# The order of a one-core attention kernel: a written table in place of a scheduler

## The chip, the cores and the metric

The kernel runs on one core of one Trainium2 chip. The metric is the device time of a run in microseconds, as the median of three runs. One profiled execution of the kernel before gives the page, the timelines and the groups of instructions quoted below. A core has five instruction queues that matter here: TensorE (PE, with its weight loads PEld), VectorE (DVE), ScalarE (ACT), GpSimd (POOL) and SyncE (SP). SP issues nearly all transfers of this kernel. Each queue runs its instructions in the order in which the program lists them, and each waits by semaphores for what it needs.

## The reference

Inputs are x of 2 x 2048 x 640, read as four sequences of 512 tokens of 640, and ctx of 2 x 128 x 384, read as four sequences of 81 tokens of 384, of which the last four are adapter tokens. All is float32, with 8 heads of 80.

```
query = x @ Wq;  keyt = enc @ Wk;  valt = enc @ Wv          # enc: the first 77 tokens, ca: the last 4
hs = mha(query, keyt, valt)
ca_q1 = einsum('btc,th->bch', ca, Wq_ca)[:, indices]        # indices = linspace(0, 383, tokens)
ca_hs1 = mha(ca_q1, x, x)
ca_hs2 = mha(ca_hs1 @ Wq, ca @ Wk_ca, ca @ Wv_ca)
out = (hs + ca_hs2) @ Wout + b_out + x
```

mha is softmax attention with scores scaled by one over the square root of 80. In the kernel the inputs are handled as two batches b of 2048 rows, with 124 keys in a padded form for the text and 384 rows of the adapter path, which a gather spreads over the tokens at the end.

## The kernel before, in words

The kernel is written as tasks. A task is a Python generator that yields operations, `Do(engine, fn, after, needs, frees, marks)`: the engine that issues it (or two engines to choose from), the function that emits its instructions, the events it waits for, the buffers it takes from a `Room`, the buffers it gives back, and the events that it marks. It can also yield a `Fork`, which begins another task. `Desk` (line 65) lists the operations in an order, calls each `fn` in turn, and pins the instructions in program order. So the order in which operations are listed is the order on each engine's queue. Instructions of DVE, ACT and POOL have the helper's line 284, PE products line 254, transposes line 269, and SP's transfers line 304.

Before the change that order is worked out when the program is built. `Desk.run` (line 205) takes, again and again, the operation that can start first by `Desk`'s own estimates of durations and landings. Among those that can start at once it takes the lowest rank: the task's rank, plus a correction from the table `RANKS`, plus a price for a change of PE's form of tile. `Room.take` hands out the buffers that came free earliest by the estimates. Where an operation may run on two engines, the one that would start it first gets it.

PE products with more than 64 rows and more than 64 columns are split by `matmul` (line 248) into four strips of 32 columns, "128*32" in the profile, unless PE is in the whole form "128*128" just then. Each float32 product of a strip shows as two records.

The work has these stages.

- First loads, weights, transposes, keys and values (to about 75 us). `keys` sends k_parts out to DRAM and reads them back in other places; `x_load(b, sb, after)` loads the eight blocks of x, `yz_block(b, sb)` makes from each the adapter's z and y, and `wq_turned` and `sums_of_wq` prepare weights.
- `adapter(b)`: for each batch 24 score products s on PE. Each is read by a maximum on DVE (mx<-s) in the first pass and by exponentials on ACT (ea<-s) in the second, and then contracted with y (acc). `second(b)` makes the adapter's second attention from that: a softmax of four on DVE and ACT, a transpose (pt_p) and a copy p2T, and then, for three blocks of 128 rows, two products (po<-w_sb,p2T), two copies o<-po on ACT, and a store o<-o by SP. p2T and the o2 tiles come from `eas`, a room of two. When second(1) is done, four PSUM banks more join the four of `banks`.
- `queries(n)` and `queries_fast(n)`: the query products pq, the later ones in a form with sums, `x_sums` and `wq_sums`, that needs fewer products. Some partial results (`rests`) go through DRAM by "away" and "landing" transfers.
- `text(m)` for 16 units m of two row tiles each: `text_scores` (sc), `softmax` on DVE, ACT and POOL (m, p, r, and the share p<-p,r on "POOL or DVE"), a DVE transpose eb, and a store kept<-eb to DRAM. `probabilities(m)` (line 1937) takes one of two pT buffers from `pTs` and reads the probabilities back in four transfers pT<-kept, each for 32 partitions. `text_out_fast` (line 2091) then does three hidden products ph (c0 = 0, 2, 4), each copied to hs by ACT or DVE. The last one gives the pT buffer back. Four sums of hs on DVE or POOL follow, and four `sums_chain` tasks with the output products po, each added by DVE onto the residual row buffer.
- `residual(m)` (line 2027) loads the two row tiles of x into two of eight row buffers (x_more and last_rows), by SP. `stored(m, k, ...)` (line 2205) runs when a tile is complete: POOL adds the adapter's rows by an indirect transfer (line 2049), and SP stores the tile, after which its row buffer is free. Tiles finished before second(b) is done are put aside to DRAM ("early") and read back later.

Each SP transfer stands in one queue with all others. A load into a buffer that an earlier transfer or product still reads makes SP wait, and with it whatever is listed behind. The lines around such a load are these:

```
op = yield Do("NONE", lambda z: wide("pT", z[0], f"pT_{m}"), needs=[(pTs, 1)], marks=[("back", m)])
for j in range(4):
    op = yield Do("SP", lambda: dma(pT[R * j : R * (j + 1)]..., by_keys[j], 1.1),
                  [("kept", m, 0), ("kept", m, 1)], rank=0)
...
op = yield Do("SP", load, [("back", m)], needs=[(rows, 1)])     # residual(m): one of two row tiles
```

Of the kernel before, what the change touches and what calls it, by code (L numbers as in the profile page):

```python
# [14 lines left out]
P = 128  # L15
# [4 lines left out]
class Event:  # L20


    def __init__(self):
        self.t = None


class Room:


    def __init__(self, n):  # L30
        self.at = [0.0] * n

    def when(self, n):
        free = sorted(t for t in self.at if t is not None)
        return free[n - 1] if len(free) >= n else None

    def take(self, n):
        order = sorted((t, i) for i, t in enumerate(self.at) if t is not None)[:n]
        for _, i in order:
            self.at[i] = None  # L40
        return [i for _, i in order]


class Do:
# [4 lines left out]
    def __init__(self, engine, fn, after=None, needs=(), frees=(), marks=(), rank=None, mode=None):  # L49
        self.engines = (engine,) if isinstance(engine, str) else engine  # L50
        self.fn, self.after, self.needs, self.frees = fn, after, needs, frees
        self.marks, self.rank, self.slots, self.value, self.mode = marks, rank, [], None, mode


class Fork:
    def __init__(self, gen, rank):
        self.gen, self.rank = gen, rank


class Task:  # L60
    def __init__(self, gen, rank, more):
        self.gen, self.rank, self.more, self.last = gen, rank, more, Event()


class Desk:
# [3 lines left out]
    ENGINES = ("PE", "ACT", "DVE", "POOL", "SP", "NONE")  # L69
    WHOLE, WIDE, SWITCH, LEAVE, ANOTHER = (P, 32), (P, None), 18.4665, -14.8473, 39.005  # L70
    START = {(P, P): 0.06, (64, P): 0.107, (P, 64): 0.107, (64, 32): 0.03, (P, 32): 0.03}
    DRAIN = {
        ((P, P), (32, P)): 0.136, ((P, P), (64, P)): 0.095, ((P, P), (P, 32)): 0.093,
        ((32, P), (P, 32)): 0.06, ((P, P), (P, P)): 0.0,
    }
    DRAINS = {(64, P): 0.148, (32, P): 0.108, (P, 32): 0.1}
    MORE = {
        "v_transpose": 0.025, "v_stream_shuffle": 0.09, "v_scalar_tensor_tensor": 0.07, "v_reciprocal": 0.035,
        "a_activation": 0.045,
    }  # L80
    COLD = 5.2
    TAIL = {"PE": 0.25, "DVE": 0.18, "ACT": 0.2, "POOL": 0.25, "SP": 0.1, "NONE": 0.0}


    RANKS = {
        "adapter": {(1,): -11.4},
        "chain": {(2, 0): 6, (2, 1): 10, (2, 2): -2, (2, 3): 19, (3, 0): -3, (3, 1): 21, (3, 2): -2, (3, 3): -2,
            (4, 1): -1, (4, 2): -0.6, (5, 0): -6, (5, 1): 20, (5, 2): -4, (5, 3): 3, (6, 0): -1, (6, 1): 16,
            (6, 3): -17, (7, 0): -3.1, (7, 1): -39.6, (7, 2): -4, (7, 3): -25},
        "context": {(): -4},  # L90
        "contract": {(0, 0): 5.7, (1, 0): -0.3, (1, 1): 5},
        "first_halves": {(): 2},
        "first_loads": {(): 1},
        "gather_rows": {(): -5},
        "halves_away": {(1,): 0.7, (3,): -1.3, (4,): 10, (5,): -2, (7,): -5},
        "keys": {(): 1.6},
        "load_wout": {(): -13},
        "probabilities": {(0,): 0.2, (1,): -4.7, (2,): -6, (3,): 7, (4,): 24.6, (5,): 11, (6,): 8.2, (7,): -23,
            (8,): 21.5, (9,): 27.1, (10,): -19.8, (11,): 25.9, (12,): 3, (13,): 16, (14,): 24.8,
            (15,): 24.7},  # L100
        "queries": {(0,): 1, (1,): -0.1},
        "queries_fast": {(2,): 36, (3,): -13, (4,): 20, (5,): 11.1, (7,): -19.7},
        "residual": {(1,): 20, (2,): -14, (3,): -1.7, (4,): -21, (5,): -8, (7,): -16, (8,): 3, (11,): 4, (13,): 15,
            (14,): 5},
        "rest_back": {(0,): 6, (1,): 20, (2,): -8.8, (3,): -10, (4,): 4, (5,): 38, (8,): 8, (10,): 10, (11,): -18.2,
            (12,): -24, (13,): 7, (14,): 2, (15,): 0.7},
        "second": {(0,): -25},
        "softmax": {(0, 0): -17.3, (0, 1): -4, (1, 0): -9, (2, 0): -7, (5, 0): -12.7, (5, 1): -20, (6, 0): -1.6,
            (6, 1): 2.1, (7, 0): -18, (7, 1): 4, (8, 0): -19, (9, 0): 8.6, (9, 1): 0.7, (10, 0): 28,
            (10, 1): 6, (11, 0): -1, (11, 1): -11.7, (12, 1): -3, (13, 0): -4, (13, 1): 10, (14, 0): -1.4,  # L110
            (15, 0): 10, (15, 1): -19},
        "stored": {(0, 0): 21, (0, 1): 12, (1, 0): -8, (1, 1): 7.2, (2, 1): 13, (3, 0): -6, (3, 1): -15, (4, 0): 2,
# [3 lines left out]
        "sums_chain": {(0, 0): -12.8, (0, 1): -4, (0, 2): 1, (0, 3): -2.3, (1, 0): -12, (1, 1): 20, (1, 2): 1.9,  # L116
# [7 lines left out]
        "sums_of_wout": {(): -2},  # L124
        "sums_of_wq": {(): 2},
        "text": {(1,): 7, (2,): -23, (3,): 12.8, (4,): 6, (5,): -10, (6,): 0.9, (7,): -1, (8,): -10, (9,): 2,
            (11,): 2.5, (12,): 11.1, (14,): -20.7, (15,): -5},
        "text_scores": {(0,): 19, (1,): -6, (2,): -17.3, (3,): 1, (5,): -10, (6,): -1, (7,): -15.8, (9,): -14,
            (12,): 6.7, (14,): 1.5, (15,): 5},
        "text_values": {(): 17},  # L130
        "values_weights": {(): 21},
        "wq_turned": {(): 4.2},
        "x_first": {(): 1},
        "x_load": {(0, 2): -4.4, (1, 1): 16, (1, 2): -20, (1, 3): 11},
        "y_rows": {(0, 0): 8, (0, 1): 16.8, (0, 2): -13, (0, 3): 34.1, (1, 0): 15, (1, 1): 8, (1, 2): -10,
            (1, 3): -1},
        "y_weights": {(): -6},
        "yz_block": {(0, 0): -40, (0, 1): -21, (0, 2): -6, (1, 0): -0.5, (1, 1): -16, (1, 2): -17, (1, 3): -22},
        "z_weights": {(): 4.9},
    }  # L140

    def __init__(self, tc):
        self.tc, self.nc, self.now, self.spent, self.mode = tc, tc.nc, 0.0, 0.0, None
        self.free = {e: 0.0 for e in self.ENGINES}
        self.queue = {e: [] for e in self.ENGINES}
        self.events, self.landed, self.channel, self.log = {}, 0.0, 0.0, []
# [4 lines left out]
    def known(self, key):  # L151
        return self.event(key).t is not None

    def begin(self, gen, rank):
        frame, key = gen.gi_frame, []
        for arg in frame.f_code.co_varnames[: frame.f_code.co_argcount]:
            if type(frame.f_locals[arg]) is not int:
                break
            key.append(frame.f_locals[arg])
        task = Task(gen, rank, self.RANKS.get(gen.__name__, {}).get(tuple(key), 0.0))  # L160
        task.last.t = self.now
        self.go_on(task, None)

    def go_on(self, task, value):
        while True:
# [6 lines left out]
            value = self.begin(op.gen, op.rank)  # L172
        op.task, op.at = task, Event()
        op.wait = [task.last] if op.after is None else [self.event(k) for k in op.after]
        op.order = task.rank if op.rank is None else op.rank
        task.last = op.at
        for e in op.engines:
            self.queue[e].append(op)

    def change(self, mode):  # L180


        if mode == self.WIDE:
            mode = self.mode if self.mode == (P, P) else self.WHOLE
# [126 lines left out]
def kernel(  # L311
# [30 lines left out]
    G = 32  # L342
# [1956 lines left out]
```

## Time and profile before

| what | value |
|---|---|
| runs | 587.95, 586.0, 587.6 us; median 587.6 |
| profiled execution | 588.24 us, its span 586.5 us |
| mean granted clock of PE | 0.997 |
| PE busy | 571.5 us, 97% of the span |
| DVE, ACT, POOL busy | 403.7, 279.1, 153.2 us |
| share of PE in the chain that ended last | 78% |
| DMA | 115.29 MB, 197 GB/s in the mean |
| SP's transfers | 64 loads pT<-kept, median 7.2 us from issue to landing; stores of rows 7.3 and 7.7 us |

How to read what is quoted. A row of the busy time by stretch gives the stretch, its length, then the busy time and the number of instructions of PE, PEld, DVE, ACT and POOL, the clock granted to PE, the share of the DMA engines and GB/s. A row of a timeline gives start, length, engine, line, operation, "out<-in", tile form (PE: rows*columns of the array that a product uses), shape and number of instructions; in brackets stands the idle time just before it and what ended it. A row of the groups gives the busy time and the mean of one in ns, and then the idle time before them. A row of the waits gives the waiting engine and line, what it waited for, the us in total, the number of times and the longest. A row of the transfers gives their number, KB each, and the median us from issue to landing.

### The profile page before, as it was taken

To read this page: it belongs to the slowest core of one execution; us is meant where nothing else is said; L and a number is where in the kernel's file an instruction comes from. 1 tells how busy PE (TensorE), PEld (TensorE's weight loads), DVE (VectorE), ACT (ScalarE), POOL (GpSimd) and SP (SyncE) were. 2 spreads that over 40 slices of the span, in tenths; PEclk is the share of its full clock that TensorE was granted. 3 is DMA by queue.
4 is the path that set the end of the run, shared out by engine and by line. 5 is a ranking of instruction groups with operands and counts; after the bars stand their busy time and mean duration, and the time that the engine had idled before them with its cause. 6 is when DMAs were issued, how large, how long until landed. Compare 5 with 4: busy or idle time off the path is not lost.

```text
span 586.5 us, 18596 instructions
## 1 busy us (share of the span) xinstructions
PE 571.5 (97%) x7913; PEld 301.2 (51%) x7913; DVE 403.7 (69%) x642; ACT 279.1 (48%) x764; POOL 153.2 (26%) x205
## 2 busy tenths in 40 slices
PE   9999999999999999999998999999999999999996
PEld 7474334545555645545544544455555564555553
DVE  2257789999999665487889999976366354444443
ACT  3132165645445789798324425269788721111110
POOL 7202031251516700000123314423213202322251
PEclk9999999999999999999998999999999999999999
DMA  8997756594868865334947999899968796799987
GB/s 274 182 247 132 155 123 205 148 201 127 161 183 168 207 147 178 103 108 151 218 129 193 281 296 229 188 270 258 293 191 168 210 257 145 185 259 260 261 173 198
DMA packets 153420, 115.29 MB, mean 197 GB/s; under 512 B 83317, under 2 KB 125685, under 8 KB 153338
## 3 DMA queue, kind: packets, MB, share of 16 engines
q1 hardware_dynamic: 147706, 103.42, 67.9%
q0 software_dynamic: 5632, 10.69, 11.0%
q8 instruction: 62, 1.02, 0.8%
q14 instruction: 20, 0.16, 0.1%
HBM read 72.54 MB, written 41.53 MB: 194 GB/s over the span
## 4 chain that ended last, share of the span: by engine, by line
PE 78%; DVE 9%; DMA 5%; ACT 5%; issue 2%; POOL 0%; SPq 0%; DVEq 0%; ACTq 0%
PE po L254 24%; PE pq L254 24%; PE ph L254 6%; PE sc L254 5%; PE s L254 5%; PE acc L254 5%; DMA kept<-eb 4%; PE pyz L254 2%; ACT ea L284 2%; DVE mx L284 2%; ACT p L284 2%; DVE eb L284 1%; PE pv L254 1%; PE pk L254 1%; DVE zop L284 1%
## 5 line engine op out<-in xcount | busy, mean ns | idle before, releaser
L284 DVE TENSOR_REDUCE mx<-s 128x4 f32<-128x2048 f32 x48 | 109.0, 2272 | 8.1 <-PE s L254 8.1
L284 ACT ACTIVATE p<-sc,m 128x124 f32<-128x124 f32 x256 | 89.9, 384 | 21.6 <-DVE m L284 21.0
L284 ACT ACTIVATE ea<-s 128x2048 f32<-128x2048 f32 x48 | 91.0, 1896 | 18.8 <-PE s L254 18.6
L254 PE MATMUL pq<-xt,wq_sb 128*32 128x256 f32 (+2 forms) x974 | 83.7, 428 | 0.0
L254 PE MATMUL po<-wout_sums,hs 128*32 128x320 f32 (+1 forms) x988 | 77.0, 433 | 0.0
L254 PE MATMUL po<-wout_sb,hs 128*32 128x320 f32 x944 | 76.0, 433 | 0.1
L284 POOL TENSOR_TENSOR p<-p,r 128x992 f32<-128x992 f32 x16 | 29.9, 1866 | 121.7 <-DVE r L284 121.7
L284 DVE TENSOR_TENSOR x_more<-x_more,po 128x320 f32<-128x320 f32 x68 | 32.3, 482 | 38.6 <-PE po L254 38.3
L284 ACT ACTIVATION_READ_ACCUMULATOR p<-sc,m 128x1 f32 x256 | 58.2, 227 | 0.0
L284 ACT COPY hs<-ph 128x512 f32<-128x512 f32 (+1 forms) x34 | 18.6, 547 | 82.3 <-PE ph L254 82.3
L254 PEld LDWEIGHTS pq<-xt,wq_sb 128*32 128x32 f32 (+1 forms) x974 | 35.6, 113 | 34.4 <-issue 18.9
L254 PE MATMUL acc<-ea,y_sb 128*32 128x384 f32 (+2 forms) x768 | 51.3, 385 | 0.0
L284 DVE TENSOR_TENSOR last_rows<-last_rows,po 128x320 f32<-128x320 f32 x60 | 28.4, 480 | 32.7 <-PE po L254 31.6
L284 DVE TENSOR_REDUCE m<-sc 128x4 f32<-128x496 f32 x64 | 40.0, 658 | 15.4 <-PE sc L254 15.4
L254 PEld LDWEIGHTS po<-wout_sb,hs 128*32 128x32 f32 x944 | 32.7, 111 | 32.6 <-issue 1.6
L254 PEld LDWEIGHTS po<-wout_sums,hs 128*32 128x32 f32 (+1 forms) x988 | 32.9, 111 | 31.9 <-issue 1.0
L254 PE MATMUL ph<-pT,vpad 128*32 128x256 f32 x768 | 47.7, 386 | 0.0
L284 DVE STREAM_TRANSPOSE eb<-p 128x1024 f32<-128x1024 f32 x32 | 39.4, 1230 | 7.2 <-DMA kept<-eb 6.9
L2049 POOL DMA_INDIRECT x_more<-o,query x16 | 24.6, 1540 | 71.5 <-DVE x_more L284 40.5
L2049 POOL DMA_INDIRECT last_rows<-o,query x16 | 25.0, 1562 | 64.5 <-DVE last_rows L284 43.3
L254 PEld LDWEIGHTS sc<-kmain,q 64*128 64x128 f32 x512 | 31.6, 187 | 15.5 <-issue 9.7
L254 PE MATMUL sc<-kmain,q 64*128 64x124 f32 x512 | 37.8, 285 | 1.3 <-DVE q L284 1.3
(210 smaller groups left out, 783.6 us busy)
## 6 DMA issues: line engine op xcount, KB each, us to landing
kept<-eb SPq DMA_DIRECT2D x32, 512.0 KB, 4.9
pT<-kept SPq DMA_DIRECT2D x64, 256.0 KB, 7.2
landing<-away SPq DMA_DIRECT2D x60, 128.0 KB, 4.0
xi<-in_x_dram SPq DMA_DIRECT2D x28, 256.0 KB, 4.9
x_more<-in_x_dram SPq DMA_DIRECT2D x17, 320.0 KB, 6.6
out_dram<-last_rows SPq DMA_DIRECT2D x16, 320.0 KB, 7.3
out_dram<-x_more SPq DMA_DIRECT2D x16, 320.0 KB, 7.7
last_rows<-in_x_dram SPq DMA_DIRECT2D x15, 320.0 KB, 8.1
```

The lines of the kernel that those rows point to most:

```text
L254: self.pin(self.nc.tensor.matmul(out[strip], lhsT[:, strip], rhs, **kw))
L284: self.pin(getattr(engine, what)(*args, **kw))
L2049: desk.pin(nc.gpsimd.indirect_dma_start(out=t, out_offset=None, in_=o2_of[b], in_offset=bass.IndirectOffsetOnAxis(ap=query[:, st : st + 1] ...
```

## The change

The scheduler, its estimates of durations and landings, the prices of a change of form, `RANKS` and all rank and mode arguments are removed. `Desk.ORDER` lists 2,259 entries, one for each operation. An entry is the number of a task in the order in which tasks were begun (a fork takes the next number when its task reaches it), and stands for that task's next operation. A letter behind it picks ACT (a), DVE (v) or POOL (g) for operations that may run on either. `Room` hands buffers out first in, first out: in the order in which the table gave them back.

The tasks are the same 539, the operations the same 2,259, and the same products and transfers are issued; but the table's order isn't the one that the scheduler had worked out. The longest common run of operations in the same order is 336 of 543 for PE, 251 for ACT, 261 for DVE, 65 for POOL and 185 of 405 for SP. Of the operations with a choice of engine 35 go from DVE to POOL, 9 from POOL to DVE, 30 from ACT to DVE and 7 from DVE to ACT; ACT has 349 operations in place of 372, DVE 560 in place of 563, POOL 123 in place of 97, and PE (543) and SP (405) as many as before.

There is one new event, "masks", marked by the sums of `masks()`. `yz_block` and the first copy of `adapter` wait for it when the order is listed. `text_out` is folded into `text_out_fast`.

```diff
 class Room:
     def __init__(self, n):
-        self.at = [0.0] * n
...
+        self.free, self.n = list(range(n)), n
     def take(self, n):
-        order = sorted((t, i) for i, t in enumerate(self.at) if t is not None)[:n]
...
+        assert len(self.free) >= n
+        taken, self.free = self.free[:n], self.free[n:]
+        return taken
+
+    def give(self, i):
+        self.free.append(i)
...
 class Desk:
-    WHOLE, WIDE, SWITCH, LEAVE, ANOTHER = (P, 32), (P, None), 18.4665, -14.8473, 39.005
...
-    RANKS = {
-        "adapter": {(1,): -11.4},
...
+    ORDER = """
+        37 0 0 2 0 4 4 0 0 0 0 0 0 0 0 0 2 2 108 4 109 0 4 2 2 2 2 2 2 110 2 2 2 2 111 112a 113v 4 0 0 0 4 4 114a 5 5
...
+        405v 414 420v 57 57 428 425v 416 89 89 97 403 403 403 403 428 81 105 93 403 418 426v 428 427v 345 421 406 423a
+        432 424g 407 422 418v 403 433v 428 403 403 429 429 421 81 431 428 405 430 431 421 430 429 421 428 421 81 81
+        428 93 89 93 93 89 345 89 406 79 93 93 432 87 89 422 87 435a 434 436v 428 429 421 81 93 421 421 421 421 421
+        421 421 421 421 421 421 421 421 421 421 442 421 407 421 434 91 421 437g 93 438v 439v 442 443 442 91 441 441
...
+        481 467 480 484v 466 479 467 488v 85 85 85 97 468 85 485 469 75 85 75 418 477 97 482 83 83 485 491 489v 77 493
+        85 487v 493 97 493 85 97 95 491 95 486v 478 497v 495 85 85 507 501 494 503v 490v 492 101 101 499v 495 504v 496
...
     def run(self):
-        while any(self.queue.values()):
...
+        for entry in self.ORDER.split():
+            task = self.tasks[int(entry.rstrip("avg"))]
+            op = task.op
+            self.engine = self.SIDES.get(entry[-1], op.engines[0])
+            assert self.engine in op.engines and all(e.known for e in op.wait), (entry, op.fn.__qualname__)
+            op.slots = [room.take(n) for room, n in op.needs]
+            op.value = op.fn(*op.slots)
+            op.at.known = True
+            for room, i in op.frees:
+                room.give(i)
+            for k in op.marks:
+                self.event(k).known = True
+            self.go_on(task, op)
...
-        yield Do("DVE", sums, ["ctx"], rank=0)
+        yield Do("DVE", sums, ["ctx"], marks=["masks"])
...
-        yield Do("NONE", lambda: None, [("x", b, sb)])
+        yield Do("NONE", lambda: None, [("x", b, sb), "masks"])
...
-            "ACT", lambda: desk.a_copy(cop[:, 0, :], ca0), [op.at] + ([("s2 half", b - 1, 0)] if b else [])
+            "ACT", lambda: desk.a_copy(cop[:, 0, :], ca0), [op.at, "masks"] + ([("s2 half", b - 1, 0)] if b else [])
...
-        pTs.at.append(op.at.t)
+        pTs.grow(1)
```

More of the change, by code (lines that the diff above doesn't have):

```diff
@@ L142, in __init__ @@
+    """
     def __init__(self, tc):
[L143 to L146, printed above, removed]
+        self.tc, self.nc, self.mode, self.events, self.tasks = tc, tc.nc, None, {}, []
     def event(self, key):
@@ L151, in known, with begin @@
     def known(self, key):
[L152 to L161, printed above, removed]
+        return self.event(key).known
+    def begin(self, gen):
+        task = Task(gen)
+        task.last.known = True
+        self.tasks.append(task)
         self.go_on(task, None)
     def go_on(self, task, value):
+        task.op = None
         while True:
@@ L171, in go_on @@
                 break
-            value = self.begin(op.gen, op.rank)
-        op.task, op.at = task, Event()
+            value = self.begin(op.gen)
+        op.at = Event()
         op.wait = [task.last] if op.after is None else [self.event(k) for k in op.after]
[L175 to L184, printed above, removed]
-        if mode is None or mode == self.mode:
-            return 0.0
-        return self.LEAVE if self.mode in (self.WHOLE, (P, P)) else self.SWITCH if mode == self.WHOLE else self.ANOTHER
@@ L221, in issue @@
-    def issue(self, t, engine, op):
-        for e in op.engines:
-            self.queue[e].remove(op)
-        self.now, self.spent, self.landed, self.engine = t, 0.0, None, engine
-        self.idle = self.free[engine] < t - 0.05
-        op.slots = [room.take(n) for room, n in op.needs]
-        op.value = op.fn(*op.slots)
-        self.free[engine] = t + self.spent if engine != "NONE" else 0.0
-        end = t + self.spent + self.TAIL[engine] if self.landed is None else self.landed
-        self.log.append((engine, t, t + self.spent, end, op.fn.__qualname__))
-        op.at.t = end
-        for room, i in op.frees:
-            room.at[i] = end
-        for k in op.marks:
-            self.event(k).t = end
-        self.go_on(op.task, op)
+        task.op, task.last = op, op.at
@@ new lines, in run @@
+    def run(self):
+        for entry in self.ORDER.split():
[11 more added lines that the diff above has]
+            self.go_on(task, op)
+        assert not any(task.op for task in self.tasks)
@@ L300, in copy, with dma @@
             self.v_tensor_copy(dst, src)
-    def dma(self, out, in_, us, issue=0.45, more=2.8):
+    def dma(self, out, in_):
         self.pin(self.nc.sync.dma_start(out, in_))
-        self.spent += issue
-        self.channel = max(self.channel, self.now + self.spent) + us
-        self.landed = self.channel + more
 @with_exitstack
@@ L1180, in queries @@
             own = [(qslots, 1)] if n not in q_of else []
[L1181 removed]
+            op = yield Do("PE", part, [*after, "wq4"], needs=[(banks, 1), *own])
             pq, s, q = op.value, op.slots[0][0], q_of[n][0]
@@ L1241, in less @@
                 )
-            yield Fork(one(Do(("POOL", "DVE"), less, after, marks=[("xs", n, i)], rank=2)), 2)
+            yield Fork(one(Do(("POOL", "DVE"), less, after, marks=[("xs", n, i)])))
         return w, b
@@ L1710, in contract @@
         yield Do(
-            "ACT", lambda: copy(accs, acc[:, :CAD]), frees=[(banks, at)], marks=[("acc done", b, j)], rank=0
+            "ACT", lambda: copy(accs, acc[:, :CAD]), frees=[(banks, at)], marks=[("acc done", b, j)]
         )
```

528 lines of the change are left out of this document (235 added, 293 removed), and 10 rows, old and new, of the table RANKS.

## The prediction

> **What bounds the kernel now.** I read the page's first part, the busy time by stretch, and then PE's timeline at its stops.
>
> ```profile
> span 586.5 us, 18596 instructions
> PE 571.5 (97%) x7913; PEld 301.2 (51%) x7913; DVE 403.7 (69%) x642; ACT 279.1 (48%) x764; POOL 153.2 (26%) x205
> ```
> ```profile
> 45.00:90.00 45.00, 43.56 (x488) 16.51 (x490) 34.92 (x49) 15.75 (x47) 6.92 (x26) 1.00 0.72 145
> 90.00:140.00 50.00, 48.38 (x668) 24.23 (x660) 49.97 (x67) 27.71 (x106) 14.89 (x9) 1.00 0.71 176
> 140.00:250.00 110.00, 109.20 (x1645) 60.93 (x1641) 82.95 (x115) 73.95 (x208) 31.12 (x33) 1.00 0.67 158
> 250.00:290.00 40.00, 38.09 (x600) 21.08 (x600) 33.81 (x45) 30.54 (x84) 3.59 (x4) 1.00 0.61 163
> 290.00:317.00 27.00, 24.22 (x298) 11.27 (x294) 22.22 (x28) 8.84 (x15) 6.56 (x6) 0.94 0.50 138
> 314.00:316.00 2.00, 2.00 (x24) 0.66 (x16) 2.00 (x2) 0.92 (x2) 0.00 (x0) 0.50 0.72 217
> 317.00:586.50 269.50, 264.23 (x3929) 138.37 (x3929) 163.10 (x272) 110.89 (x283) 73.24 (x57) 1.00 0.91 230
> ```
> ```profile
> 82.78 1.05 PE L254 MATMUL pyz<-xt,wyz 64*32 64x512 f32 x4 [1.10 <-DVE wq_sums L284]
> 309.67 1.23 PE L254 MATMUL sc<-kmain,q 64*128 64x124 f32 x14 [1.27 <-DVE q L284]
> 312.86 0.64 PE L269 MATMUL pt_p<-ident,p2pad 128*113 128x128 f32 x3 [1.35 <-DVE p2pad L284]
> 578.91 2.88 PE L254 MATMUL po<-wout_sb,hs 128*32 128x320 f32 x40
> ```
>
> PE bounds it: busy for 571.5 of 586.5 us. The first number behind each stretch is PE's busy time. From 45 to 317 PE idles 1.44 + 1.62 + 0.80 + 1.91 + 2.78 = 8.55 us, in stops of which the longest, 1.1 to 1.35 us, wait for DVE, and after the last two stops the granted clock, the number behind the busy times, is 0.50 in 314 to 316; its mean of 0.94 over 290 to 317 loses 27 x 0.06 = 1.6 us. From 317 on it idles 5.3 us, of which 4.7 follow its last matmuls (578.91 + 2.88). So the reloads, stores and additions of the last 270 us are wholly hidden today. An order can win little; it can lose what that hiding is worth.
>
> **The change part by part.** The same 539 tasks and 2,259 operations are issued, and the table can be read entry by entry: an entry is the number of a task in order of begin and stands for its next operation. Distances in "us of PE work" are PE's products between two entries, at the durations of the rows.
>
> *Early stops.* The table issues the keys' reloads before x_load(0, 3), and yz_block(0, 1) earlier; it puts other PE work between the steps of second(0), and no read of scores, DVE's or ACT's pass and reuse of its bank stand closer than about 1 us of PE work. What this can win is bounded by 8.55 us plus the 1.6 of the clock: 0 to 10.2. Most of the stops named above lose their cause, so I take 8. If their covers fail, the next to be late is DVE, full in 90:140 (49.97 of 50).
>
> *PE's form of tile.* Departures from 128*32 tiles fall from 115 to 105.
>
> ```profile
> 128.18 1.92 PE L254 MATMUL pq<-xt,wq 128*32 128x512 f32 x16
> 130.04 0.51 PE L254 MATMUL s<-zop,cop 32*128 32x512 f32 x4
> 130.47 1.92 PE L254 MATMUL pq<-xt,wq 128*32 128x512 f32 x16
> 132.22 1.05 PE L254 MATMUL pq<-x_sums,wq_sums 128*32 128x256 f32 x16
> ```
>
> The same 16 matmuls take 1.86 us to the next start before a change of form and 1.75 without: 0.11 each, 1.1 us in all (0 to 1.1, where a stop covers it). Deleting the scheduler costs nothing on the chip.
>
> *Probabilities' buffers, the large term.* pT has two buffers; unit m's last hidden product (c0 = 4) frees one, SP then reloads it in four transfers, and the next unit's hidden products wait for all four.
>
> ```profile
> 466.78 1.84 SPq L304 DMA_DIRECT2D pT<-kept x4
> ```
> ```profile
> 482.69 1.07 PE L254 MATMUL ph<-pT,vpad 128*32 128x256 f32 x16
> 507.39 1.05 PE L254 MATMUL ph<-pT,vpad 128*32 128x256 f32 x16
> 508.25 0.72 PE L254 MATMUL po<-wout_sb,hs 128*32 128x320 f32 x8
> 508.79 1.91 PE L254 MATMUL ph<-pT,vpad 128*32 128x256 f32 x32
> 510.52 1.26 PE L254 MATMUL po<-wout_sb,hs 128*32 128x320 f32 x16
> ```
> ```profile
> SPq L304 <- PE ph L254: 37.9, 9, 12.2
> SPq L304 <- DMA out_dram<-last_rows: 20.6, 10, 3.9
> SPq L304 <- DMA out_dram<-x_more: 13.9, 7, 4.1
> ```
> ```profile
> pT<-kept SPq DMA_DIRECT2D x64, 256.0 KB, 7.2
> out_dram<-last_rows SPq DMA_DIRECT2D x16, 320.0 KB, 7.3
> out_dram<-x_more SPq DMA_DIRECT2D x16, 320.0 KB, 7.7
> o<-o SPq DMA_DIRECT2D x6, 320.0 KB, 3.9
> ```
> ```profile
> L304 SPq DMA_DIRECT2D pT<-kept x64: 302/431/1878, 276.9 to 549.7; - x64
> DMA to landing us min/median/max: 4.5/7.2/12.2
> ```
>
> Unit 12 is the tightest today: SP, which had waited for ph, starts its loads at 466.78, and its products start at 482.69, 15.9 us later. A release needs 4 x 0.46 (1.84 for four) + 7.2 = 9.0 us. In the table unit 12 takes unit 4's buffer, released 24 us of PE work before use, and unit 13 takes unit 10's, although it is computed first. Between unit 10's last hidden product and unit 13's first stands one chain step of 8 matmuls: 0.54 us (508.25 to 508.79). The entries are "81 81 428 93 89 93 93 89 345 89 406 79 93 93" (probabilities(m) is task 41 + 4m, residual(m) 39 + 4m; 428 is the chain step): the first 93 takes the buffer, then SP issues loads of units 12, 13, 13, 12, the store of [2, 1] (345), 12, the store of [6, 0] (406), the second row load of residual(10), 13, 13. That row load takes the row buffer of [2, 1], so SP stands in it until that store lands. Worked out: store [2, 1] issued after 4 x 0.46 = 1.8, landed at 1.8 + 7.3 = 9.1; then 13's two last loads, 0.9; then 7.2: 17.2, less 0.54 is 16.7 us of stopped PE. If the store does not hold SP and the loads take their shortest 4.5: 9 issues, 4.1 + 4.5 - 0.54 = 8.1. I take 13, nearer the middle, since the medians were measured in a stretch with the DMA engines 91% busy.
>
> *second(1) behind it.* The table puts its six products (task 421; 0.54 us each by the rows above) directly after 13's first, and today they stand apart:
>
> ```profile
> 480.43 0.70 PE L254 MATMUL po<-w_sb,p2T 113*128 113x320 f32 x2
> 482.05 0.70 PE L254 MATMUL po<-w_sb,p2T 113*128 113x320 f32 x2
> ```
> ```profile
> L284 ACT COPY o<-po 128x320 f32<-128x320 f32 x12 | 5.1, 426 | 25.1 <-PE po L254 23.7 <-issue 1.4
> ```
>
> One ea buffer holds p2T, so three o2 tiles share the other: two round trips of store and landing (0.3 + 3.9 each) with six copies of 0.43 make 11.0 us, with four banks and about 5.2 us of PE work queued against it: 5.8, with bounds 0 (the copies had been done) and 8 (SP later still). I take 5. ACT's next copy (unit 13's) and, on SP, the rows of unit 13 queue behind it.
>
> *Unit 11.* It takes unit 9's buffer with a chain step of 24 matmuls and one of 16 between, 1.6 + 1.07 = 2.7 us. The entries of SP "85 85 97 468 85 469 75 85" are loads of 11, 11, 14, the store of [10, 1], 11, the store of [10, 0], residual(9)'s first row load, which waits for the store of [10, 1], then 11: 3 x 0.46 + 7.7 + 0.46 + 7.2 = 16.7, less 2.7 is 14.0; unblocked and at the shortest, 7 x 0.46 + 0.46 + 4.5 - 2.7 = 5.5. I take 11. Behind it four more row loads stand one to three entries after the store whose buffer they take, some 8 us of SP each, before unit 15's loads: 9.5 + 32 + 7.2 = 49 us from the release until these land, against 16.7 + 33 us of PE work when its products come. Even: 1 (0 to 3).
>
> *The clock.* After the 1.3 us stops at 309 and 312 the clock was 0.50 at 314. Three stops of 5 us and more should each cost about the 1.6 us above: I take 4 (0 to 5). [...]
>
> *Engines chosen.* 35 operations go from DVE to POOL and 9 back, 30 from ACT to DVE and 7 back; PE and SP keep their counts.
>
> ```profile
> L284 POOL TENSOR_TENSOR hs<-hs 128x256 f32<-128x256 f32 x20 | 16.0, 800 | 34.4 <-ACT hs L284 23.3 <-DVE r L284 7.6 <-DVE hs L284 2.8
> L284 POOL TENSOR_TENSOR p<-p,r 128x992 f32<-128x992 f32 x16 | 29.9, 1866 | 121.7 <-DVE r L284 121.7
> ```
> ```profile
> 75.53 0.38 DVE L284 TENSOR_TENSOR wq_sums<-wq_sb 128x256 f32<-128x256 f32 x1
> 77.69 1.51 DVE L284 TENSOR_TENSOR wq_sums<-wq_sb 128x256 f32<-128x256 f32 x1
> ```
> ```profile
> 77.13 1.78 POOL L284 TENSOR_TENSOR x_sums<-xt 128x512 f32<-128x512 f32 x1 [1.97 <-ACT rests L284]
> ```
>
> POOL gains 26, most of them hs sums of 0.80, five shares of 1.87. POOL and DVE have room where most of them lie (73 and 163 of the last 269.5 us), so 0; the cost if not is the second rival.
>
> *The new wait* for "masks" concerns work done in the first microseconds: 0, and a few tenths of a us if the masks came late.
>
> *Sum,* against the profiled execution's 588.2 us (span 586.5 and 1.7 around it), which stands 0.6 above the median of 587.6: 588.2 - 8 - 1.1 + 13 + 5 + 11 + 1 + 4 = 613.1, less 0.6: about 612 us. All terms at their low ends give 588.2 - 10.2 - 1.1 + 8.1 + 5.5 = 590.5; at their high ends 588.2 + 16.7 + 8 + 14 + 3 + 5 = 635. The first is taken up below; for the second all would have to fall together.
>
> **The rivals.**
>
> *Faster, 578.* One mechanism: unit 13 or 11 does not take the buffer I assign to it, for instance because units 12 and 13 are the other way round. Then 24 us stand between release and use, over the 9.0 needed, and 588.2 - 9.1 - 0.6 = 578.5. It decides at 9.0 us of distance. For it: the early part of the table is so consistently better; today all distances exceed 15. Against: with two buffers, first in, first out, and unit 13's loads entered after unit 10's release, no other buffer is free.
>
> *The same, 588: DVE locked by POOL.* The wq_sums operation takes 0.38 us at 75.53 and 1.51 us at 77.69, where POOL's sums of x run beside it. If the late stops don't come, but the five shares of 1.87 us (9.3 us) hold DVE in the stretch where it has no idle time, the early gain of 9.1 is gone: 588.2 - 9.1 + 9.3 - 0.6 = 587.8. It decides when the locked time exceeds the gain. [...]
>
> *Slower by little, about 591.* The stops come at their low ends, since SP isn't held by the stores: 590 to 594. For it: landings go down to 4.5 us; against: SP did wait 17 times on such landings.
>
> *Nothing but the changes of form:* 587.6 - 1.1 = 586.5, if stops only move.
>
> **How the numbers follow.** Forecast 0.72 (its own range 594 to 628); little slower 0.07; faster 0.14; DVE locked 0.05; nothing 0.02. A difference under 0.3% (1.8 us) is not told from no change in this kernel. Slower is 0.72 + 0.07 = 0.79, the same 0.07, faster 0.14. The range is 580 to 628: about half of the faster case lies below it, and little of the forecast above.
>
> **What would show it.** Right: on PE's timeline a stop of 8 to 17 us before a ph in the last 130 us, another of 5 to 14 some 50 us of work later, released by the DMA pT<-kept; SP's waits on out_dram landings above 34.5 us in all; a clock of 0.50 after each. PE's busy time by stretch before 317 idle by 0.5 to 3 us in all in place of 8.55. Wrong: ph follows the release without such a stop, or early stops of a new kind (a score product waiting for DVE beside POOL's p) appear.

## The result, and the profile after

The changed kernel takes 649.0 us (median of four runs, 648.7 to 650.3) against 586.9 us before: a ratio of 1.106, with a 95% interval of 1.1035 to 1.1088. It was forecast slower and is slower, but by 62 us in place of 25, outside the range of 580 to 628. The profiled execution has a span of 647.1 us.

The page's first part, after:

```profile
span 647.1 us, 18547 instructions
PE 583.4 (90%) x7907; PEld 305.9 (47%) x7907; DVE 400.6 (62%) x640; ACT 265.4 (41%) x740; POOL 179.9 (28%) x231
```

The same products kept PE busy for 583.4 us in place of 571.5, and PE was idle for 63.7 us in place of 15.0. So of the 60.6 us by which the span grew, 48.7 are idle time of PE and 11.9 are longer busy time for the same products. The busy time by stretch, after (the first number behind the length is PE's busy time, the three numbers at the end are PE's clock, the DMA share and GB/s):

```profile
45.00:90.00 45.00, 45.00 (x565) 18.84 (x561) 35.03 (x56) 19.11 (x62) 4.61 (x19) 1.00 0.69 142
90.00:140.00 50.00, 43.73 (x552) 20.80 (x550) 43.09 (x53) 21.09 (x82) 13.91 (x10) 0.93 0.51 124
140.00:250.00 110.00, 109.66 (x1669) 61.60 (x1667) 87.48 (x122) 71.93 (x208) 36.46 (x36) 1.00 0.75 181
250.00:290.00 40.00, 38.66 (x600) 21.05 (x600) 27.92 (x39) 31.62 (x84) 7.52 (x6) 1.00 0.39 119
290.00:317.00 27.00, 26.78 (x369) 13.23 (x361) 24.85 (x28) 10.78 (x25) 11.98 (x12) 1.00 0.60 158
317.00:400.00 83.00, 76.30 (x997) 38.97 (x989) 70.90 (x89) 32.13 (x119) 25.12 (x23) 0.96 0.87 218
500.00:550.00 50.00, 38.31 (x536) 17.54 (x540) 12.60 (x27) 4.88 (x11) 7.95 (x8) 0.84 0.60 162
550.00:600.00 50.00, 28.12 (x356) 13.18 (x352) 13.06 (x28) 0.00 (x0) 8.38 (x6) 0.74 0.70 171
```

From 45 to 317 PE idles 0 + 6.27 + 0.34 + 1.34 + 0.22 = 8.2 us, against 8.55 before. The gain was there in four stretches (0 for 1.44, 0.34 for 0.80, 1.34 for 1.91, 0.22 for 2.78), and the fifth, 90:140, took it back (6.27 for 1.62), most of it in one stop. PE's timeline at its long stops, after:

```profile
102.39 3.64 PE L211 MATMUL pq<-x_sums,wq_sums 128*32 128x256 f32 x32 [5.10 <-DVE q L226]
350.44 3.43 PE L211 MATMUL po<-wout_sb,hs 128*32 128x320 f32 x24 [6.70 <-ACT o L226]
507.75 1.93 PE L211 MATMUL ph<-pT,vpad 128*32 128x256 f32 x16 [16.98 <-DMA pT<-kept]
515.05 0.74 PE L211 MATMUL po<-w_sb,p2T 113*32 113x320 f32 x8 [1.25 <-ACT o L226]
519.56 1.94 PE L211 MATMUL ph<-pT,vpad 128*32 128x256 f32 x16 [2.69 <-ACT o L226]
563.21 1.93 PE L211 MATMUL ph<-pT,vpad 128*32 128x256 f32 x16 [8.64 <-DMA pT<-kept]
590.95 1.94 PE L211 MATMUL ph<-pT,vpad 128*32 128x256 f32 x16 [10.69 <-DMA x_more<-in_x_dram]
595.43 1.94 PE L211 MATMUL ph<-pT,vpad 128*32 128x256 f32 x16 [2.54 <-DMA pT<-kept]
```

Counted along PE's order, these are: queries_fast(2), a PSUM bank that second(0) holds, unit 13, second(1) twice, unit 9, unit 11 (the trace names a row load as what ended it; that it is the reload of pT is read from the order, and from e3 below) and unit 14. They add up to 54.6 us. SP's waits, after:

```profile
SPq L236 <- PE ph L211: 63.2, 9, 14.4
SPq L236 <- DMA out_dram<-x_more: 21.5, 6, 5.8
SPq L236 <- DMA out_dram<-last_rows: 21.0, 7, 5.8
```

SP stood 63.2 us for a release by ph in place of 37.9, and 42.5 us for stores in place of 34.5. SP's timeline around unit 13 shows both, after:

```profile
490.29 1.38 SPq L236 DMA_DIRECT2D pT<-kept  x3
491.78 0.37 SPq L236 DMA_DIRECT2D out_dram<-last_rows  x1
492.19 0.46 SPq L236 DMA_DIRECT2D pT<-kept  x1
493.06 0.36 SPq L236 DMA_DIRECT2D out_dram<-last_rows  x1
499.23 0.35 SPq L236 DMA_DIRECT2D last_rows<-in_x_dram  x1
499.64 0.90 SPq L236 DMA_DIRECT2D pT<-kept  x2
```

SP stood for 5.8 us (493.06 + 0.36 to 499.23) in the row load. By the table it takes the row buffer that the store at 491.78 gives back, and it was issued 7.45 us after that store. Unit 13's last two loads stand behind the row load, and its products start 7.2 us after these are issued. The stop at 102 is not SP's. DVE's timeline ahead of it, after:

```profile
95.28 2.49 DVE L226 STREAM_TRANSPOSE xt<-xi 128x512 f32<-128x512 f32 x4 [8.43 <-PE pq L211]
98.36 1.20 DVE L226 STREAM_TRANSPOSE eb<-p 128x1024 f32<-128x1024 f32 x1
99.48 2.25 DVE L226 TENSOR_REDUCE mx<-s 128x4 f32<-128x2048 f32 x1
101.66 0.67 DVE L226 COPY q<-pq 128x512 f32<-128x512 f32 x1
```

DVE stood for 8.43 us in the transposes of x_load(0, 3), which write an xt buffer that queries(1) still read. Six operations of DVE stand between these transposes and the next one of x_load(0, 3); when they are listed first (e4 below), they run between 86.5 and 95.9 us, in the time in which DVE stood here. At 350 ACT waits for an o2 buffer, whose store SP had issued at 341.39:

```profile
341.39 0.34 SPq L236 DMA_DIRECT2D o<-o  x1
```
```profile
349.96 0.75 ACT L226 COPY o<-po 128x320 f32<-128x320 f32 x2 [8.01 <-DMA o<-o]
```

By the table PE's next product takes the PSUM bank that the first of these two copies frees, so PE stops with it. Here no operation of ACT that was ready is seen behind the wait; on SP and DVE there was. These two queues each stood at an entry that wasn't ready, with work behind it that was. The clock after the stop of 16.98 us, from the busy time in windows of 2 us:

```profile
507.00:509.00 2.00, 1.25 (x12) 0.68 (x16) 0.00 (x0) 0.00 (x0) 0.00 (x0) 0.50 0.95 243
509.00:511.00 2.00, 2.00 (x20) 0.90 (x16) 0.00 (x0) 0.14 (x1) 0.00 (x0) 0.50 0.61 184
511.00:513.00 2.00, 2.00 (x24) 0.94 (x20) 0.00 (x0) 0.71 (x2) 0.00 (x0) 0.64 0.00 0
```

### The profile page after: what moved, and what is told of

It reads as the page before. It is cut to its first block, busy times and chain, and to the rows that moved or that the text cites. A ratio compares the mean times of both kernels' runs of the same rounds, so it can differ in the third digit from the quotient of the medians.

```text
span 647.1 us, 18547 instructions
## 1 busy us (share of the span) xinstructions
PE 583.4 (90%) x7907; PEld 305.9 (47%) x7907; DVE 400.6 (62%) x640; ACT 265.4 (41%) x740; POOL 179.9 (28%) x231
## 3 DMA queue, kind: packets, MB, share of 16 engines
q0 software_dynamic: 5632, 10.69, 9.5%
## 4 chain that ended last, share of the span: by engine, by line
PE 73%; DMA 11%; DVE 8%; ACT 3%; issue 2%; SPq 2%; DVEq 0%; ACTq 0%
PE po L211 22%; PE pq L211 19%; PE ph L211 7%; PE acc L211 6%; PE sc L211 6%; PE s L211 5%; DMA pT<-kept 4%; DVE mx L226 2%; DMA o<-o 2%; SPq L236 2%; PE pyz L211 2%; DMA zb<-z 1%; ACT ea L226 1%; ACT p L226 1%; DMA out_dram<-last_rows 1%
## 5 line engine op out<-in xcount | busy, mean ns | idle before, releaser
L211 PE MATMUL ph<-pT,vpad 128*32 128x256 f32 x768 | 52.6, 412 | 41.5 <-DMA pT<-kept 28.2
L211 PE MATMUL po<-wout_sb,hs 128*32 128x320 f32 (+1 forms) x996 | 83.0, 445 | 6.7 <-ACT o L226 6.7
L211 PE MATMUL po<-wout_sums,hs 128*32 128x320 f32 (+1 forms) x928 | 79.3, 444 | 0.0
L226 POOL TENSOR_TENSOR p<-p,r 128x992 f32<-128x992 f32 x21 | 39.0, 1857 | 127.4 <-DVE r L226 127.0
L226 POOL TENSOR_TENSOR hs<-hs 128x256 f32<-128x256 f32 x36 | 29.8, 835 | 96.4 <-ACT hs L226 65.4
L226 ACT ACTIVATION_READ_ACCUMULATOR p<-sc,m 128x1 f32 x256 | 56.1, 219 | 0.0
L211 PEld LDWEIGHTS ph<-pT,vpad 128*32 128x32 f32 x768 | 25.2, 117 | 64.6 <-issue 43.9
L211 PEld LDWEIGHTS po<-wout_sb,hs 128*32 128x32 f32 (+1 forms) x996 | 35.5, 114 | 42.1 <-ACT o L226 7.5
L1971 POOL DMA_INDIRECT last_rows<-o,query x17 | 26.9, 1580 | 61.8 <-DVE last_rows L226 20.2
L226 ACT COPY hs<-ph 128x512 f32<-128x512 f32 (+1 forms) x25 | 12.9, 530 | 69.8 <-PE ph L211 48.8
```

The costliest lines, as they stand in the source:

```text
L211: self.pin(self.nc.tensor.matmul(out[strip], lhsT[:, strip], rhs, **kw))
L226: return lambda *args, **kw: self.pin(getattr(engine, what)(*args, **kw))
L1971: desk.pin(nc.gpsimd.indirect_dma_start(out=t, out_offset=None, in_=o2_of[b], in_offset=bass.IndirectOffsetOnAxis(ap=query[:, st : st + 1] ...
```

## The experiments

In the edits an entry's task is named in place of its number. The joint is the place in a mixed table where one order hands over to the other; half clock is time at a granted clock of 0.50. The medians of the kernel before, run beside them, are 588.2 (e1 to e4), 587.4 (e5 to e8), 587.1 (e9 to e12) and 587.3 us (e13, e14).

**Is it the order?** e1 has the old order in the new form.

```diff
-    ORDER = """ (the table)
+    ORDER = """ (the order and the engines that the scheduler had worked out, entry by entry)
```

> The table holds the order and the engines that the scheduler had worked out; buffers are still handed out first in, first out, and nothing is estimated. If the order on the queues is all that costs, the time is that of the kernel before, 587 us within 2, with 64 loads pT<-kept and no stop of PE over 1.5 us after the first 5 us. If the handing out of buffers first in, first out costs by itself, buffers change hands and stops of several us appear: 595 or more.

Measured: 587.6 us, 0.9995 of before (0.998 to 1.001). The form of the program and the handing out of buffers first in, first out cost nothing; all 62 us are the order, the choice of engines included.

**Early or late?** e5 and e8 take one part from each.

```diff
+    ORDER = """ e5: the table's order for the scheduler's first 1,800 operations, then the scheduler's for 459
+    ORDER = """ e8: the scheduler's order for the table's first 1,800 operations, then the table's for 459
```

> The table's own order for the operations that the scheduler had listed among its first 1,800, and the scheduler's order and engines for the 459 behind them. If the six late stops (16.98, 1.25, 2.69, 8.64, 10.69, 2.54: 42.8 us) and the half clock after them (some 9 us of PE's longer busy time) come from the order of the last part alone, they go: 649 - 43 - 9 = 597, with the stops at 102 (5.10) and 350 (6.70) left. If they are prepared earlier, by row or pT buffers that come free late, stops of 5 us and more stay behind 450 and the time is over 610.

> The reverse of e5_late_before: the scheduler's order for the operations that the table lists among its first 1,800, and the table's for the rest. If the parts add up, early and late: 588 + 43 + 9 = 640, with the stops ahead of units 13, 9, 11 and 14 within 1.5 us of those of the changed kernel. If the late stops need the early order's delays, under 620.

Measured: e5 602.0 us, 14.6 above the kernel before; e8 635.9, 48.5 above. Together 63.1, against 62.1 for the whole change: the parts add up. In e5 the late stops are gone and one at the joint is new (the first row). In e8 those of units 13, 9 and 11 (the other rows) are within 1.1 us of those of the changed kernel.

```profile
470.52 1.64 PE L211 MATMUL po<-wout_sums,hs 128*32 128x320 f32 x16 [4.02 <-DVE x_more L226]
```
```profile
497.17 1.93 PE L211 MATMUL ph<-pT,vpad 128*32 128x256 f32 x16 [15.89 <-DMA out_dram<-last_rows]
549.88 1.94 PE L211 MATMUL ph<-pT,vpad 128*32 128x256 f32 x16 [8.28 <-DMA pT<-kept]
579.23 1.94 PE L211 MATMUL ph<-pT,vpad 128*32 128x256 f32 x16 [11.33 <-DMA last_rows<-in_x_dram]
```

**The buffer, or SP's queue?** e2 changes who takes which buffer and puts the loads of each of the two units together; e3 changes only SP's order.

```diff
 e2: -prob(12) takes ... prob(13) takes, SP: 12 13 13 12 store 12 store row(10) 13 13 ... 12
     +prob(13) takes, SP: 13 13 13 13 ... prob(12) takes, SP: 12 12 12 12 store store row(10)
 e3: -SP: 12 13 13 12 store 12 store row(10) 13 13 ... 12
     +SP: 13 13 13 13 12 12 12 12 store store row(10)
     -SP: 14 9 14 9 9 9 ... 11 11 14 store 11 store row(9) 11 ... 14
     +SP: 9 9 9 9 14 14 ... 11 11 11 11 14 14 store store row(9)
```

> The changed kernel, but unit 13 takes unit 4's pT buffer and unit 12 takes unit 10's; each one's four loads stand together, 13's right behind its taking. If the stop of 16.98 us ahead of unit 13's hidden products is the reload of a buffer released 0.54 us of PE work earlier, it goes with some 2 us of half clock: 649 - 17 - 2 = 630, with the stops behind second(1) (1.25 and 2.69), unit 9 (8.64), 11 (10.69) and 14 (2.54) left as they are. If SP as a whole is late there, the stop moves to unit 12 and the time stays above 643.

> The changed kernel with nothing but SP's order changed in the last part: the four loads of units 13, 12, 9, 11 and 14 stand together, ahead of the stores and row loads, and unit 9's ahead of unit 14's; every buffer is the same. If SP standing in row loads and in loads for buffers not yet released is what makes the stops so long, they shrink to the release alone: unit 13 4 x 0.46 + 7.3 - 0.54 = 8.6 in place of 16.98, unit 9 none in place of 8.64, unit 11 1.8 + 7.3 - 2.7 = 6.4 in place of 10.69, unit 14 none in place of 2.54: 24 us less and some 4 of half clock, 621. If only the release counts, the stops at 13 and 11 stay and the time is about 640.

Measured: e2 643.8 us, just inside its second expectation, but the stop moved to second(1) and not to unit 12; e3 635.8, between its two. PE's timeline of e2, then of e3:

```profile
507.68 1.30 PE L211 MATMUL po<-w_sb,p2T 113*32 113x320 f32 x8 [15.66 <-ACT o L226]
```
```profile
500.18 1.93 PE L211 MATMUL ph<-pT,vpad 128*32 128x256 f32 x16 [8.09 <-DMA pT<-kept]
515.84 1.30 PE L211 MATMUL po<-w_sb,p2T 113*32 113x320 f32 x8 [9.48 <-ACT o L226]
576.07 3.64 PE L211 MATMUL ph<-pT,vpad 128*32 128x256 f32 x32 [7.64 <-DMA pT<-kept]
```

With its loads together, unit 13 stands 8.09 us (8.6 worked out) in place of 16.98, unit 9 not at all, and units 11 and 14 together 7.64 in place of 13.2 (6.4 worked out for 11). So about half of the stops at 13 and 11 was the release standing too near its use, and half of them, with all of unit 9's, SP standing in other entries. But neither time came down by as much as its stops: in both second(1) stands 9.5 to 15.7 us, where it had stood 3.9. Its stores o<-o are on the same queue behind the same row loads; in e2 the first two copies that they store were done at 490.9, and the first store was issued only at 502.2:

```profile
502.22 6.08 SPq L236 DMA_DIRECT2D o<-o  x2
```

Unit 13's stop had hidden that wait. e9 puts these stores ahead.

```diff
 e9: as e2 and e3, and
-SP: 12 12 12 12 store store row(10) store row(12) store row(12) o2 o2 store o2
+SP: 12 12 12 12 store store store store o2 o2 row(10) store o2 row(12) row(12)
```

> The changed kernel with the late part mended in its own order: the pT buffers of units 12 and 13 changed over, the loads of 13, 12, 9, 11, 14 each together, unit 9's ahead of 14's, and on SP the stores o<-o of second(1) ahead of the row loads that wait for stores. If SP's order is what stops PE: no stop at 13, at second(1) the two round trips alone (4 to 6 in place of 15.66 in e2_swap_12_13), no stop at 9, about 7.6 at 11 and 5 behind it as in e3_loads_first: 649 - 24 - 3 of half clock = 622. If the row loads, now later, stop DVE's additions instead, 630 or more.

Measured: 626.7 us, between its two expectations, and second(1) still stands 11.77 us. SP's timeline, then ACT's, of e9:

```profile
495.76 9.80 SPq L236 DMA_DIRECT2D o<-o  x2
```
```profile
504.45 0.75 ACT L226 COPY o<-po 128x320 f32<-128x320 f32 x2 [12.41 <-DMA o<-o]
```

The first o<-o was issued at 495.8 and released ACT at 504.5: 8.7 us, where the median from issue to landing before was 3.9. Eight transfers, unit 12's four loads and four stores of rows, had been issued in the 7 us ahead of it. SP's order within the late part, with the change of buffers between units 12 and 13, explains 22 us of the 48.5 (649.0 to 626.7). What is left there, the two round trips of second(1) from store to copy, the release of unit 11's buffer and additions that wait for late row loads, went only in e5, which has the old order and engines on every queue; which of these it takes was not tried.

**The early stops.** e4 moves the transposes alone; e6 is e5 with them and second(0) moved.

```diff
 e4: -DVE: x_load(0,3) x4, then six other operations
     +DVE: the six other operations, then x_load(0,3) x4
 e6: e5 with e4's move, and the second and the third block of second(0) each put off by some 8 us of PE work
```

> The changed kernel with four DVE operations moved: the transposes x_load(0, 3) that wait for the last product of queries(1) stand behind the nine DVE operations that were listed after them. If DVE stood in that wait with ready work behind it, the stop of 5.10 us at 102 and the half clock after it go: 649 - 5 - 2 = 642. If DVE is simply short of time there (it was busy for 49.97 of 50 us from 90 to 140 in the kernel before), another stop for DVE follows within 20 us and the time stays within 2 us of 649.

> As e5_late_before, and with two mends of the early part: the transposes x_load(0, 3) behind the ready DVE work as in e4_turns_later, and the products and copies of second(0)'s second and third block put off by some 8 us of PE work, so that each stands about 9 us behind the store whose buffer it takes. If these two waits are all that the early order loses, the gain forecast for it is seen: 597 - 9 - 6.7 - 1.5 = 580, some 7 us under the kernel before. If the early order gains nothing, 587 or more.

(The expectation of e4 counts nine operations of DVE; the table has six.) Measured: e4 639.7 us, 9.3 less than the changed kernel, where 7 were expected. Of this 3.8 us are the stop at 102, which fell from 5.10 to 1.34; the half clock behind it went too (the mean clock of 90:140 is 1.00, where it was 0.93), and two later stops are shorter (5.40 us in place of 6.70 for second(0), 15.79 in place of 16.98 for unit 13), which was not expected. e6 takes 591.4 us, 10.5 less than e5 (9 + 6.7 + 1.5 expected). PE's timeline at 102 in e4, and what is left at the joint in e6:

```profile
102.24 3.01 PE L211 MATMUL pq<-xt,wq_sb 128*32 128x256 f32 x52 [1.34 <-DVE wq_sums L226]
```
```profile
460.57 2.36 PE L211 MATMUL po<-wout_sums,hs 128*32 128x320 f32 x16 [3.23 <-DVE x_more L226]
```

**The engines.** e7 puts the table's choice into the scheduler's order, e10 the scheduler's choice into the table's.

```diff
 e7:  the scheduler's entries, letters a, v, g as in the table
 e10: the table's entries, letters a, v, g as the scheduler had chosen
```

> The scheduler's order with the table's choice of engine for the operations that may run on two: 35 from DVE to POOL, 9 back, 30 from ACT to DVE, 7 back. If the choice costs nothing: 587.5 within 2. If DVE and POOL exclude each other, or POOL's longer times (1.86 against DVE's 1.19 for a share) delay the stores of probabilities, up to 9.3 us more: 590 to 597.

> The table's order with the scheduler's choice of engine for every operation that may run on two. e7_engines_after has the choice cost 15 us in the scheduler's order. If that is the price of the choice itself, it comes off here: 634. If a choice fits its order, and the price is that of any mixture, no gain: 645 or more, with the late stops as in the changed kernel.

Measured: e7 602.8 us, 15.4 above the kernel before and more than either expectation; e10 668.0, 19 above the changed kernel. Neither choice is the worse by itself: each is slower in the other's order. By the profiles PE is idle 7.1 us longer in e7 than before and busy 7.9 us longer. Its one long stop, on PE's timeline and then POOL's:

```profile
574.10 2.36 PE L211 MATMUL po<-wout_sb,hs 128*32 128x320 f32 x16 [6.28 <-POOL hs L226]
```
```profile
567.81 1.54 POOL L1971 DMA_INDIRECT last_rows<-o,query  x1 [14.65 <-DMA last_rows<-in_x_dram]
568.79 1.99 POOL L226 TENSOR_TENSOR hs<-hs 128x256 f32<-128x256 f32 x2
```

The sums of hs, given to POOL, stand behind an addition that waits 14.65 us for its row load. It is the same mechanism on a third queue. Where e10's 19 us arise was not taken apart.

**Is there an early gain at all?** e11 and e12 cut at other places.

```diff
 e11: the table's order for the scheduler's first 1,240 operations, x_load(0,3)'s transposes four DVE operations later than in e6
 e12: the same for the first 1,560, with second(0) put off as in e6
 e13: e11 with e6's place of the transposes; on ACT the copy p2T ahead of a cast of rests
 e14: e6 with the last DVE transpose eb behind three additions of unit 5
```

> The table's order only for the operations that the scheduler had listed among its first 1,240 (to about 294 us of PE work, ahead of second(0)), with the transposes x_load(0, 3) four DVE operations later still than in e6_mended; the scheduler's order behind. If the early order is worth what the windows of e6_mended up to 290 show (PE idle 4.1 us there against 5.8, and two stops fewer at 309 and 312 if the rest shifts with it) and nothing is lost at the joint: 583 to 586. If the joint itself costs, as the stop of 3.23 us at 460 in e6_mended, 588 or more.

> As e11_early_294, but the table's order for the scheduler's first 1,560 operations (to about 362 us), with second(0) put off as in e6_mended. If the gain lies in the stretch from 290 to 317 as well (0.2 us of PE idle in e6_mended against 2.8, and no half clock): 581 to 584, under e11_early_294. If the joint costs, 588 or more.

Measured: e11 589.5 us (1.0049 of before, 1.0027 to 1.007) and e12 594.7 (1.0121, 1.0087 to 1.0155). Each has one long stop at its joint, e11 3.92 us behind ACT's p2T, e12 7.96 us behind POOL's hs. In e11 the copy p2T stands on ACT behind a cast that waits 5.17 us for a landing transfer: the same mechanism on a fourth queue.

> As e11_early_294, but the copy p2T of second(0) stands on ACT ahead of the cast of rests that waits for a landing transfer (PE stood 3.92 us behind that copy), and the transposes x_load(0, 3) stand where e6_mended has them. If the early order gains what was forecast from 45 to 317: 589.5 - 3.9 - 1.5 of half clock = 584, 0.5% under the kernel before. If the early order gains nothing, another stop takes the place and it is 587 or more.

> As e6_mended, but the last DVE transpose eb, which waits 7.59 us for the store kept<-eb, stands behind the four additions of unit 5 that were listed after it (PE stood 3.23 us behind them). If that wait alone was the loss at the joint: 591.4 - 3.2 - 2.5 of half clock = 586, 0.2% under the kernel before, the same within what can be told. If the additions stand behind something else, 590 or more.

Measured: e13 588.2 us (1.002, 1.0005 to 1.0034): the stop moved to the additions, as in the second expectation. e14 585.6 us, 0.9964 of the kernel before (0.9947 to 0.998). (Its expectation names four additions; the transpose goes behind three.) The two rows are e13's and e14's longest stops behind 300:

```profile
322.42 2.36 PE L211 MATMUL po<-wout_sums,hs 128*32 128x320 f32 x16 [4.12 <-DVE x_more L226]
```
```profile
342.53 0.77 PE L211 MATMUL s<-zop,cop 32*128 32x512 f32 x4 [2.27 <-DVE mx L226]
```

e14 is the only version whose interval lies below the kernel before, once both early waits and the one at the joint are mended and the late order is the old one. But its 1.7 us are less than the 1.8 that the prediction set as the least to be told from no change, and the profiled execution of e14 took 588.0 us, so its rows don't show a gain. Stops of 1.34 and 2.27 us are still in it; how much would be gained without those wasn't tried. The early order gains little, if anything.

## Why the prediction was right in direction and wrong in size

- *Early stops, 8 us of gain: this step failed.* Idle time from 45 to 317 went from 8.55 to 8.2 us, where 0.5 to 3 was the sign of being right, and the mean clock in 90:140 fell to 0.93 (an estimated loss of 50 x 0.07 = 3.5 us). The step measured distances on PE's own order, from product to product, and took the other queues as ready. It didn't ask what stands behind the transposes of x_load(0, 3) on DVE while they wait for the last product of queries(1): 8.43 us on DVE, 5.10 of them on PE, and e4 with them moved is 9.3 us faster. Even then PE idles 4.4 us from 45 to 317, so the stops that could be won were about 4 us and not 8.
- *second(0): the same step, the wrong way round.* Other PE work between its steps was counted as a gain. The table puts that work ahead of the store o<-o and none behind it, so the copies that reuse the o2 buffer came right after the store: 6.70 us at 350.
- *Unit 13: the mechanism held, the term was too small.* 13 was taken, 16.98 measured; the sum worked out in the text, 16.7, was right, and the reason for going below it (landings on an emptier queue) was not. By e3 the release accounts for 8.1 of it; the rest, 8.9, is what SP issues between, with its wait of 5.8 us for the store.
- *Unit 11 and second(1): right in number.* 10.69 against 11, and 3.9 against 5. But e2, e3 and e9 show that second(1) was small only because unit 13's stop lay over it, so that number is in part luck. The 1 us was set for unit 15, which did not stop; unit 14, which the sum did not have, stood 2.54.
- *Unit 9: left out of the sum without a reason given, 8.64 us.* Its own buffer is released 29 us of PE work ahead, wide enough by itself. Its loads stand behind one of unit 14, which waits for unit 8's release. No distance was read for the queue; in e3, with unit 9's loads ahead of unit 14's, the stop is gone.
- *The clock: 4 us forecast, for three stops.* There were eight, and PE's busy time rose by 11.9 us for the same products. Behind the stops at 102, 350, 507 and 563 PE worked for 3.8 to 5.0 us at 0.50 (the 16 matmuls ph at 507.75 took 1.93 us, those at 603.54, at 1.00, took 1.05). About 4 us of such work is an estimated 2 us of loss each time, so six such stops would make it. The form of tile (1.1 us of gain) can't be seen beside that.
- *Rivals.* That buffers fall otherwise was wrong: unit 13 did take unit 10's. A slower DVE beside POOL is in the trace, but small: DVE's shares p<-p,r took 1.41 us in place of 1.19 and its sums of hs 0.52 in place of 0.45, some 4.5 us over 39 operations, while mx (2.28 and 2.27) and the additions from PSUM (0.48 both) took the same.

```profile
L226 DVE TENSOR_TENSOR p<-p,r 128x992 f32<-128x992 f32 x11 | 15.5, 1413 | 0.1
```
```profile
L284 DVE TENSOR_TENSOR p<-p,r 128x992 f32<-128x992 f32 x16 | 19.1, 1191 | 0.5
```

The first row is after, the second before. The rise of the shares lies in two of the eleven, beside which an operation of POOL had begun 0.2 to 0.4 us earlier: 1.91 us at 234.75 beside x_sums, and 2.97 at 396.37 beside POOL's own share. The other nine took 1.18 or 1.19. In one of these, at 442.28, DVE had begun first, and POOL's sum of hs beside it took 1.54 us, where these sums take 0.84 in the mean. Of the share of 2.97 us, DVE and then POOL:

```profile
396.37 2.97 DVE L226 TENSOR_TENSOR p<-p,r 128x992 f32<-128x992 f32 x1
```
```profile
396.18 2.10 POOL L226 TENSOR_TENSOR p<-p,r 128x992 f32<-128x992 f32 x1
```

That this had any part in the stops is not shown. One reading of the prediction was off without changing a term: of the stops of 1.1 to 1.35 us before 317, the one of 1.22 at 264.71 waits for ACT and not for DVE.

Put together: 8 + 1.1 of gain that didn't come (the 5.1 at 102 are in it), 6.7 at 350, 4 more at unit 13, 8.6 at unit 9, 1.5 at units 14 and 15, some 8 more for the clock, less 1 at second(1): 37 us, by which the forecast of 612 was short.

## What to carry to other kernels

When an order is written out by hand, read each queue by itself: for every entry that may wait, ask what that wait is for, when it ends, and which ready entries stand behind it. A reuse distance that looks wide for the buffer says nothing if the reload is queued behind another reload that isn't released. A wait that lies under a longer one has no price in the trace, so mending the longest stop brings less than its length; here 17 us of stop were worth 5 (e2).

## What was not expected of the hardware

- Behind the stops of 5.10, 6.70, 16.98 and 8.64 us PE's clock was granted at 0.50 for 3.8 to 5.0 us of work; behind the one of 10.69 us, which unit 14's of 2.54 us follows, it was 0.50 up to 601. In the stretches above its mean is under 1 only where such stops lie (0.93, 0.96, 0.84, 0.74). Shorter stops were followed by a low clock too: before, two of 1.27 and 1.35 us within 5 us by 0.50 in 314:316; after, those of 1.25 and 2.69 us by 0.56 and 0.58 in 519:521 and 521:523.
- In e9 a store o<-o of 320 KB took 8.7 us to release the copy that waited for it, with eight transfers issued in the 7 us ahead of it; the one at 341.39 in the changed kernel took 8.6 us. The median from issue to landing before was 3.9. So moving these stores ahead on SP (e9) brought less than their place in the order had cost; that the transfers in front were the reason was not tried.
